# Gathering the chosen tokens with a bfloat16 one-hot matrix and three bfloat16 pieces, split on GpSimd

## The chip, the cores and the metric

The kernel runs on one core of a Trainium2 chip. The metric is device microseconds of one execution, as the median of several runs. The profile is one more execution, taken by the hardware profiler. Engine names in it: PE is the TensorE matmul, PEld its weight load, DVE is VectorE, ACT ScalarE, POOL GpSimd, SP the engine whose queue issues most DMAs.

## The reference, cut to what matters

Four sequences of 512 tokens with 128 features pass through two "layers". The first has three attention parts, two of them with a mixture of eight experts behind them. The second is a block with chosen tokens, four layers of additive attention, and the block with chosen tokens again. The change lies in that block (`k` is 512 / 8 = 64 tokens for each of 8 experts):

```python
logits = sigmoid(einsum('bth,eh->bte', X, Wr))
topk_vals, topk_I = top_k(logits.transpose(0, 2, 1), k)
idx_flat = topk_I.reshape(B, E * k)
Xg = take_along_axis(X, idx_flat[:, :, None], axis=1).reshape(B, E, k, H)
QKV = einsum('beki,eij->bekj', Xg, Wqkv)
Q, K, V = split(QKV, 3)
# rotary angles of the tokens' own places on 64 columns of Q and K
M = topk_I[..., :, None] >= topk_I[..., None, :]
A = softmax(where(M, Q @ K^T / sqrt(128), -inf))
AV = (A @ V) * topk_vals[..., None]
out[b, idx_flat] += AV @ Wo
```

So each expert takes its 64 best tokens out of 512, lets them attend to one another, and adds the result back to the rows that they came from. X is layer-normalized first, and half of the block's output is added to the residual stream.

## The kernel before, in words

Everything is float32 and stays in SBUF. A batch (one sequence) is four chunks of 128 tokens. The work is written as generators, each `yield` a step. `in_turn` and the loops of `first_layer` take steps from several generators in turn, and a scheduler then fixes one order of instructions for each engine. In that order each engine works strictly: an instruction that waits holds up all behind it on its engine. PSUM banks are given out by `bank()` by an estimate of when each comes free.

The block with chosen tokens runs twice: once from about 820 to 980 us of the profile (called the first part below; its beginning overlaps the end of the last mixture of experts) and once from about 1235 us to the end (the last part). Each time, two choices are made, each for two batches at once:

- `choice` (L778 to L856) loads the table `m_trig` (cosines, sines and the token's number) into the columns behind the 128 features of a tile `m_yg` (L785, SP's queue), normalizes X into the tile's first 128 columns (moments L790; `r` on POOL, L154; L182), transposes (L803) and multiplies by the router's weights (L809), forms the sigmoid (`gates`, L819 to L822), transposes it to 16 rows of 512 (L827, L829) and copies it on POOL into the last 8 columns of `m_yg` (L831). So a row of `m_yg` has 201 columns: everything that is to be gathered of a token. Then eight rounds of MAX8 (L836) and MATCH_REPLACE8 (L838) on DVE mark the 64 best, a scan (L846) numbers them, and a transposition (L852, L854) gives `byt`: for each token and expert the slot that it has there, or 0.
- `stream` (L862, one for each batch) makes the one-hot matrix `pick` by comparing `byt` with the slots' numbers (L869, DVE) and gathers by matmul (L880): for each pair of experts and each chunk, `pick` is the stationary operand (128x128) and `m_yg` the moving one (128x201). The gathered rows go to `xs` (L887), are transposed to `xg` (L890), and POOL and DVE take out the chosen token's own gate (`own` L892, `gate` L894). Then come QKV (L903), the rotary part (DVE L915 to L918, POOL's `qk` addition L921 with the tile `other`, two buffers), the transposes of q and k, scores (L931, L932; L932 is the only bf16 matmul of the kernel), softmax, `back` (L952), AV (L961, `av` L964), the output projection (L970) and the one-hot matmul back to the tokens (L983), added to X at L992.
- `chosen_attention` steps both choices and the four streams in turn; a stream starts when its batch is chosen and the stream before it has made five steps.

Beside the first choice of the first part runs the end of the last mixture of experts: `gates` (L673 to L746) computes which two experts a token goes to. In it POOL multiplies and adds two small comparison tables (L712, L718), DVE reduces them to a `rank` (L725) and weights `comb` (L731 to L737), PE transposes those (L741), a DMA puts them to DRAM (L745, `away`) and eight DMAs broadcast them back (L458, `spread`). Each half of an expert is then a matmul (L267), a tanh (L467), a product on DVE (`v`, L472), a product with `spread` on POOL (`hid`, L473) and a second matmul into a sum (L267).

In the last part, the first choice (batches 0 and 1) runs beside the last steps of the additive attention of batches 2 and 3. POOL adds their result to X (L1266), and the second choice's moments (L167) read it.

Of the kernel before, what the change touches and what calls it, by code (L numbers as in the profile page):

```python
# [8 lines left out]
F32 = mybir.dt.float32  # L9
BF16 = mybir.dt.bfloat16  # L10
AF = mybir.ActivationFunctionType
ALU = mybir.AluOpType
AX = mybir.AxisListType

P = 128
B = 4
NC = 4
T = NC * P
# [5 lines left out]
NE = 8  # L24
FH = 2
KSEL = T // 8
# [5 lines left out]
AT_T, AT_G, YG = P + NROT, P + NROT + 1, P + NROT + 1 + NE  # L32
# [8 lines left out]
def tile_macaron(ctx: ExitStack, tc: tile.TileContext, a: dict, out: bass.AP):  # L41
    nc = tc.nc
# [10 lines left out]
    def bank(hold=1.6):  # L53
        i = min(range(8), key=lambda i: free[i])
        free[i] = max(free[i], clock[0]) + hold
        return psum[i].tile([P, T], F32, tag="bank", name="bank")
# [166 lines left out]
    for i in range(4):  # L223
        e = slice(2 * i, 2 * i + 2)
# [7 lines left out]
    def first_layer(opened, picked):  # L232
        with (
# [532 lines left out]
            streaming.close()  # L766
            top = opened()
            choosing = choice([0, 1], lambda b: (1, b) in mixed, top, picked)
            while background or beside or mixing or made:
                halves[0] += 1  # L770
# [7 lines left out]
    def choice(batches, done, top, picked):  # L778
# [1 line left out]

        R = NE * len(batches)
        n = NC * R
        ygs = [top.tile([P, NC, YG], F32, name=f"m_yg{b}") for b in batches]
        for yg in ygs:
            nc.sync.dma_start(yg[:, :, P:AT_G], a["m_trig"].rearrange("(c p) j -> p c j", p=P))  # L785
        while not all(done(b) for b in batches):
# [42 lines left out]
        nc.vector.tensor_copy(left, pr[0:R, :])  # L829
        for i in range(len(batches)):  # L830
            nc.gpsimd.tensor_copy(ygs[i][:, :, AT_G : AT_G + NE], gates[:, :, i * NE : (i + 1) * NE])  # L831
        yield

        for i in range(KSEL // 8):
# [18 lines left out]
        byt = top.tile([P, NC, R], F32, name="byt")  # L853
        nc.vector.tensor_copy(byt, pt[:, 0:n].rearrange("p (c r) -> p c r", c=NC))  # L854
        for i, b in enumerate(batches):
            picked[b] = ygs[i], byt[:, :, i * NE : (i + 1) * NE]  # L856

    def chosen_attention(top, picked, choosing, beside=()):

        with tc.tile_pool(name="moa", bufs=2) as wp:  # L860

            def stream(b):  # L862

                yg, byt = picked[b]

                pick = wp.tile([P, NC, NE, KSEL], F32, name="pick")
                for c in range(NC):
                    at = byt[:, c, :].unsqueeze(2).to_broadcast([P, NE, KSEL])
                    nc.vector.tensor_tensor(  # L869
# [5 lines left out]
                for k in range(2):  # L875
                    ps = bank().rearrange("p (i n) -> p i n", i=2)
                    for i in range(2):
                        r = 2 * k + i
                        for c in range(NC):
                            nc.tensor.matmul(  # L880
                                ps[:, i, 0:YG],
                                lhsT=pick[:, c, 2 * r : 2 * r + 2, :].rearrange("p e s -> p (e s)"),
                                rhs=yg[:, c, :],
                                start=(c == 0),
                                stop=(c == NC - 1),
                            )
                    (nc.scalar.copy if k else nc.vector.tensor_copy)(xs[:, 2 * k : 2 * k + 2, :], ps[:, :, 0:YG])  # L887
                    yield
                xg = wp.tile([P, T], F32, name="xg")
# [9 lines left out]
                for r in range(NPAIR):  # L899
                    ps = bank()  # L900
                    for i in range(2):
                        e = 2 * r + i
                        nc.tensor.matmul(  # L903
                            ps[i * KSEL : (i + 1) * KSEL, 0 : 3 * P],
                            lhsT=xg[:, e * KSEL : (e + 1) * KSEL],
                            rhs=late["m_wqkv"][:, e, :],
                            start=True,
                            stop=True,
# [51 lines left out]
                for r in range(NPAIR):  # L960
                    nc.tensor.matmul(  # L961
                        pav[:, r * P : (r + 1) * P], lhsT=v[:, r, :], rhs=eT[:, r, :], start=True, stop=True
                    )
                av = wp.tile([P, T], F32, name="av")  # L964
                nc.scalar.copy(av, pav)
                yield
                pw = bank()
                for e in range(NE):
# [3 lines left out]
                        lhsT=av[:, e * KSEL : (e + 1) * KSEL],  # L972
                        rhs=late["m_wo"][:, e, :],
                        start=True,
                        stop=True,
# [5 lines left out]
                for c in range(NC):  # L981
                    for r in range(NPAIR):
                        nc.tensor.matmul(  # L983
                            po[:, c * P : (c + 1) * P],
                            lhsT=back[:, r, c * P : (c + 1) * P],
                            rhs=xp[:, r, :],
                            start=(r == 0),
                            stop=(r == NPAIR - 1),
# [3 lines left out]
                nc.vector.scalar_tensor_tensor(X[:, b], by_chunk(po), 0.5, X[:, b], ALU.mult, ALU.add)  # L992

            others = choice([2, 3], lambda b: True, top, picked)
            steps = [0] * B

            def behind(b):

                while b not in picked or (b > 0 and steps[b - 1] < 5):
                    yield  # L1000
                for _ in stream(b):
                    steps[b] += 1
                    yield
                steps[b] += 5
# [101 lines left out]
    def additive_attention(opened, picked, weights, ready):  # L1106

        A = 2 * P
        with tc.tile_pool(name="add", bufs=2) as wp, tc.tile_pool(name="one", bufs=1) as hp:
# [162 lines left out]
            runs += [(STEPS * (i - 1) + 15, weights(i)) for i in range(1, DEPTH)]  # L1272
            top = opened()
            choosing = choice([0, 1], lambda b: b in finished, top, picked)
            last = runs[B - 1][1]
            ended = []
# [16 lines left out]
    with ExitStack() as until_chosen:  # L1293
# [6 lines left out]
        wp, ready = until_done.enter_context(made), {}  # L1300
# [75 lines left out]
```

## Time and profile before

| | |
|---|---|
| time, median of 3 runs | 1371.02 us (1368.14 to 1375.04) |
| the profiled execution's own span | 1369.7 us, 29349 instructions |
| PE busy | 1289.1 us (94%) |
| DVE busy | 954.4 us (70%) |
| ACT busy | 586.5 us (43%) |
| POOL busy | 562.1 us (41%) |
| chain that ended last, by engine | PE 13%, DVE 10%, POOL 4% of the span as merged lines |
| the gather matmuls L880 | 256 records, 0.333 us each by the median, from 888.8 to 1338.3 |

How to read it: the busy time of PE is of modelled ends, and its matmuls overlap, so the time that a matmul takes from PE is the distance between two starts, not its duration. A line of the timeline is: start (us), time until the end of the group (us), engine, line of the kernel, operation, output<-inputs, shapes, count, and in brackets how long the engine sat idle before it and what ended that. A line of the groups is: line, engine, operation, names, shapes, count | busy us, mean ns of one | idle before.

### The profile page before, as it was taken

What the parts mean: (1) busy time and instruction counts of PE and PEld (TensorE: products, weight loads), DVE (VectorE), ACT (ScalarE), POOL (GpSimd) and SP (SyncE); (2) the same over time, 40 slices, a digit from 0 to 9 for tenths busy, and PEclk for the clock granted to TensorE, in tenths of its full rate; (3) what the DMA queues carried; (4) which work ended last, traced back from release to release, by engine and by line L of the source; (5) the groups of instructions that cost most, each with busy time, mean ns of one, the idle gap of its engine ahead of it and who ended that gap; (6) DMA issues with size and microseconds to landing.
All of it is one profiled execution on the core that took longest, in us unless ns stands there. A gap on an engine that the chain in (4) does not pass through costs nothing. (4 is left out here: it accounts for less than half of the span.)

```text
span 1369.7 us, 29349 instructions
## 1 busy us (share of the span) xinstructions
PE 1289.1 (94%) x11050; PEld 699.9 (51%) x11050; DVE 954.4 (70%) x3293; ACT 586.5 (43%) x1180; POOL 562.1 (41%) x823
## 2 busy tenths in 40 slices
PE   5998999999999999999999999989889999997897
PEld 2554445333333333465544443367667767665675
DVE  6886776666658777778767638687466776667773
ACT  1555454454556666665545443222223332323222
POOL 8345655544424112024564755622244443543100
PEclk8999999999999999999999999999979999999799
DMA  3001101020111100000111011211000100000000
GB/s 115 21 24 41 43 33 49 2 80 1 64 45 32 39 1 18 3 19 19 50 33 34 33 53 28 76 40 40 1 20 5 40 1 17 1 1 1 1 9 23
DMA packets 37172, 39.52 MB, mean 29 GB/s; under 512 B 11080, under 2 KB 23880, under 8 KB 37032
## 3 DMA queue, kind: packets, MB, share of 16 engines
q1 hardware_dynamic: 34536, 35.06, 8.3%
q10 hardware_dynamic: 2496, 2.59, 0.6%
q8 instruction: 87, 1.43, 0.4%
q14 instruction: 53, 0.43, 0.1%
HBM read 29.45 MB, written 1.18 MB: 22 GB/s over the span
## 5 line engine op out<-in xcount | busy, mean ns | idle before, releaser
L574 ACT ACTIVATE e<-bank 128x512 f32<-128x512 f32 x576 | 313.7, 595 | 278.4 <-PE bank L527 240.0
L527 PE MATMUL bank<-kA,qA 32*128 32x512 f32 (+3 forms) x1536 | 349.0, 527 | 4.1 <-DVE nm L543 1.8
L562 PE MATMUL bank<-qA,kA 32*128 32x512 f32 (+3 forms) x1536 | 334.0, 524 | 0.3 <-DVE nm L543 0.3
L543 DVE CUSTOM_DVE_ANT_0 junk<-bank,causal 128x384 f32<-128x384 f32 (+3 forms) x512 | 251.0, 490 | 89.5 <-PE bank L527 51.3
L547 DVE TENSOR_REDUCE nm<-bank 128x1 f32<-128x512 f32 x256 | 164.9, 686 | 78.9 <-PE bank L527 78.7
L473 POOL TENSOR_TENSOR hid<-v,spread 128x512 f32<-128x512 f32 x128 | 163.9, 1286 | 127.1 <-DVE v L472 101.7
L562 PEld LDWEIGHTS bank<-qA,kA 32*128 32x128 f32 x1536 | 129.5, 185 | 136.9 <-issue 54.1
L605 PE MATMUL sum<-e,vA 128*32 128x256 f32 (+1 forms) x2560 | 183.7, 368 | 6.1 <-POOL e L580 6.0
L580 POOL TENSOR_SCALAR_AFFINE_SELECT e<-e 128x256 f32<-128x256 f32 x256 | 99.3, 407 | 192.8 <-ACT e L574 191.7
L527 PEld LDWEIGHTS bank<-kA,qA 32*128 32x128 f32 x1536 | 147.4, 187 | 24.6 <-DVE nm L543 5.8
L605 PEld LDWEIGHTS sum<-e,vA 128*32 128x32 f32 x2560 | 62.8, 109 | 165.8 <-issue 134.0
L267 PE MATMUL sum<-hid,sb_f_w 128*32 128x512 f32 x1024 | 135.6, 597 | 3.0 <-POOL hid L473 2.9
L267 PE MATMUL bank<-tT,sb_f_w 128*32 128x512 f32 x1024 | 137.1, 602 | 0.0
L472 DVE SCALAR_TENSOR_TENSOR v<-th,bank 128x512 f32<-128x512 f32 x128 | 87.0, 681 | 43.9 <-ACT th L467 29.2
L467 ACT ACTIVATE th<-bank 128x512 f32<-128x512 f32 x128 | 76.3, 597 | 49.0 <-PE bank L267 39.5
L154 POOL TENSOR_TENSOR r<-v,mhalf 128x4 f32<-128x4 f32 (+1 forms) x64 | 71.8, 1123 | 5.1
L1250 PE MATMUL bank<-h2T,w 128*128 128x512 f32 x128 | 69.0, 632 | 0.2 <-ACT h2T L1239 0.2
L1256 PE MATMUL bank<-w,hid 128*128 128x128 f32 x512 | 65.7, 277 | 0.1
L1256 PEld LDWEIGHTS bank<-w,hid 128*128 128x128 f32 x512 | 63.1, 194 | 4.8 <-issue 1.5
L1251 ACT ACTIVATE hid<-bank,sb_l_cols 128x512 f32<-128x512 f32 x64 | 43.9, 688 | 39.9 <-PE bank L1250 39.8
L1148 PE MATMUL bank<-wa,hT 128*128 128x385 f32 x128 | 56.5, 540 | 1.4 <-ACT hT L1141 1.4
L312 POOL TENSOR_SCALAR v<-mv 128x4 f32<-128x4 f32 x12 | 2.8, 230 | 131.1 <-DVE mv L171 130.8
(279 smaller groups left out, 1805.4 us busy)
## 6 DMA issues: line engine op xcount, KB each, us to landing
spread<-away SPq DMA_DIRECT2D x64, 256.0 KB
qA<-mT SPq DMA_DIRECT2D x192, 2.0 KB
qA<-qC SPq DMA_DIRECT2D x11, 256.0 KB
kA<-kC SPq DMA_DIRECT2D x11, 256.0 KB
w<-in_l_w_dram SPq DMA_DIRECT2D x8, 256.0 KB
sb_m_wqkv<-in_m_wqkv_dram SPq DMA_DIRECT2D x4, 384.0 KB
m_yg<-in_m_trig_dram SPq DMA_DIRECT2D x8, 130.0 KB
X<-in_x_dram SPq DMA_DIRECT2D x4, 256.0 KB
```

Source lines behind the costliest of these rows:

```text
L267: nc.tensor.matmul(ps[32 * j : 32 * j + 32, :], lhsT=w[:, 32 * j : 32 * j + 32], rhs=rhs, start=start, stop=stop, skip_group_check=True,)
L467: nc.scalar.activation(th, ph, AF.Tanh, scale=0.5)
L472: nc.vector.scalar_tensor_tensor(v, th, 1.0, ph, ALU.add, ALU.mult)
L473: nc.gpsimd.tensor_tensor(hid, v, self.spread[e], op=ALU.mult)
L527: nc.tensor.matmul(ps[:, at : at + w], lhsT=t.qA[r0 : r0 + 32, g, c * P : (c + 1) * P], rhs=t.kA[r0 : r0 + 32, g, 0:w], start=True, stop=True,
L543: nc.vector.tensor_tensor_reduce(junk[:, 0:w], src, causal[:, T - w : T], 1.0, NEG, ALU.add, ALU.max, dst)
L547: nc.vector.tensor_reduce(dst, src, axis=AX.X, op=ALU.max)
L562: nc.tensor.matmul(ps[:, at : at + w], lhsT=t.kA[r0 : r0 + 32, g, kc * P : (kc + 1) * P], rhs=t.qA[r0 : r0 + 32, g, q0:T], start=True, sto ...
L574: nc.scalar.activation(es[n][:, j, :], ps, AF.Exp)
L580: nc.gpsimd.affine_select(out=e, in_=e, pattern=[[0, 2], [1, P]], compare_op=ALU.is_ge, fill=0.0, base=0, channel_multiplier=-1,)
L605: nc.tensor.matmul(to[32 * j : 32 * j + 32, q0 + lo - at : q0 + hi - at], lhsT=t.vA[:, kc, 4 * j + g, :], rhs=es[n][:, j, lo:hi], start=fresh,
L1256: nc.tensor.matmul(pm[:, c * P : (c + 1) * P], lhsT=hid[:, f, c * P : (c + 1) * P], rhs=w2[:, f, :], start=(f == 0), stop=(f == 3),)
```

## The change

The gather matmul becomes bfloat16, without loss: each row of `m_yg` is split into three bfloat16 pieces whose sum is the float32 row. The first piece is the row rounded to bfloat16; the rest (float32) is rounded to the second; what is left is the third. `pick` is 0 or 1 and is written as bfloat16. Each f32 matmul becomes three bf16 ones into the same sum.

The split is done on POOL in `choice`, right behind the copy of the gates and ahead of the eight rounds: for each batch and each two chunks (128x402) a conversion, a subtraction, a conversion, a subtraction. `rest` lies in the buffer of `yT` (tag), so a second split of a batch waits for the first. The tiles `m_yg` are now named by their place in a choice and no more by the batch, so the second choice's tiles use the buffers of the first one's and wait until those have been read. The pieces have tiles of their own for each batch. `av` shares the two buffers of `xg`.

In the instruction order of the changed kernel POOL's new operations of the two batches are interleaved with one another and with what POOL did there before.

```diff
-        ygs = [top.tile([P, NC, YG], F32, name=f"m_yg{b}") for b in batches]
+        ygs = [top.tile([P, NC, YG], F32, name=f"m_yg{i}") for i in range(len(batches))]
+        pieces = [[top.tile([P, NC, YG], BF16, name=f"m_p{b}{s}") for s in range(3)] for b in batches]
+
+        def split(i):
+
+            for c in range(0, NC, 2):
+                x, of = [p[:, c : c + 2] for p in pieces[i]], ygs[i][:, c : c + 2]
+                rest = top.tile([P, T], F32, tag=f"yT{i}", name="rest")[:, 0 : 2 * YG].rearrange("p (c n) -> p c n", c=2)
+                nc.gpsimd.tensor_copy(x[0], of)
+                nc.gpsimd.tensor_tensor(rest, of, x[0], op=ALU.subtract)
+                nc.gpsimd.tensor_copy(x[1], rest)
+                nc.gpsimd.tensor_tensor(x[2], rest, x[1], op=ALU.subtract)
+
...
         for i in range(len(batches)):
             nc.gpsimd.tensor_copy(ygs[i][:, :, AT_G : AT_G + NE], gates[:, :, i * NE : (i + 1) * NE])
+        for i in range(len(batches)):
+            split(i)
         yield
...
         for i, b in enumerate(batches):
-            picked[b] = ygs[i], byt[:, :, i * NE : (i + 1) * NE]
+            picked[b] = pieces[i], byt[:, :, i * NE : (i + 1) * NE]
...
-                yg, byt = picked[b]
-
-                pick = wp.tile([P, NC, NE, KSEL], F32, name="pick")
+                pieces, byt = picked[b]
+
+                pick = wp.tile([P, NC, NE, KSEL], BF16, name="pick")
...
                         for c in range(NC):
-                            nc.tensor.matmul(
-                                ps[:, i, 0:YG],
-                                lhsT=pick[:, c, 2 * r : 2 * r + 2, :].rearrange("p e s -> p (e s)"),
-                                rhs=yg[:, c, :],
-                                start=(c == 0),
-                                stop=(c == NC - 1),
-                            )
+                            for k3, piece in enumerate(pieces):
+                                nc.tensor.matmul(
+                                    ps[:, i, 0:YG],
+                                    lhsT=pick[:, c, 2 * r : 2 * r + 2, :].rearrange("p e s -> p (e s)"),
+                                    rhs=piece[:, c, :],
+                                    start=(c == 0 and k3 == 0),
+                                    stop=(c == NC - 1 and k3 == 2),
+                                )
...
-                av = wp.tile([P, T], F32, name="av")
+                av = wp.tile([P, T], F32, tag="xg", name="av")
```

## The prediction, made before the changed kernel had run

> **What bounds it now.** First I read the page's strip of busy tenths, then the timeline around the two places where tokens are chosen (about 815 to 960 us and 1235 us to the end), engine by engine.
>
> ```profile
> span 1369.7 us, 29349 instructions
> PE   5998999999999999999999999989889999997897
> POOL 8345655544424112024564755622244443543100
> ```
>
> TensorE is the bound nearly everywhere, so cheaper gather matmuls should count. GpSimd (POOL) looks half idle. But a queue that is half idle on average can be the one thing waited for in one stage. So next the stage in which the change gives POOL work, the timeline of POOL, DVE and PE after the first choice:
>
> ```profile
> 839.72 0.36 POOL L831 COPY m_yg<-gates 128x32 f32<-128x32 f32 x2
> 840.33 1.27 POOL L473 TENSOR_TENSOR hid<-v,spread 128x512 f32<-128x512 f32 x1 [0.25 <-DVE v L472]
> 841.80 1.27 POOL L473 TENSOR_TENSOR hid<-v,spread 128x512 f32<-128x512 f32 x1 [0.19 <-DVE v L472]
> 844.35 0.73 POOL L712 TENSOR_TENSOR same<-same,before 128x256 f32<-128x256 f32 x1 [1.29 <-DVE same L711]
> 845.16 0.72 POOL L718 TENSOR_TENSOR more<-more,same 128x256 f32<-128x256 f32 x1
> ```
>
> ```profile
> 846.52 0.40 DVE L725 TENSOR_REDUCE rank<-more 128x32 f32<-128x256 f32 x1
> ...
> 852.29 0.17 DVE L737 TENSOR_TENSOR comb<-comb,rs 128x32 f32<-128x32 f32 x1
> ```
>
> ```profile
> 852.51 0.60 PE L741 MATMUL bank<-ident,comb 128*8 128x128 f32 x4 [0.62 <-DVE comb L737]
> ```
>
> The reader is to see a chain: the expert gates of the last mixture pass POOL (L712, L718), then DVE, then PE, then a DMA, and only at 858.75 can POOL multiply its first `hid`. From L831 to L718 POOL idles 1.7 us in all. There is no room for a split there.
>
> **PE: the gather.** 128 f32 matmuls (8 batches x 4 pairs x 4 chunks, two records each) become 384 bf16 ones.
>
> ```profile
> 951.09 3.00 PE L880 MATMUL bank<-m_yg,pick 128*128 128x201 f32 x16
> ...
> 1343.98 0.22 PE L932 MATMUL bank<-paired,ident_h 128*128 128x128 bf16 x1
> 1344.03 0.44 PE L931 MATMUL bank<-kT,qT 128*128 128x128 f32 x2
> ```
>
> Sixteen records need 2.93 us to the next group's start; inside a group a record starts 0.17 us after the other (1335.94, 1336.11, 1336.28), so a matmul takes 0.34. A bf16 matmul of 128 columns has the next one start 0.055 us later; for 201 columns 0.086, three 0.258. Saved: 0.082. The bf16 weight load is a record of 0.10 us against 0.19 for f32, so I count it as hidden under the matmul before it. That is 1.3 us a batch: 2.6 for each two batches at full clock, but 3.3 for the two behind 1277.1, where the first 32 records took 8.29 us at a granted clock of 0.5. Sum 11.2 saved, taken whole, since PE runs without gaps there. Ends: 0.055 a piece (201 columns no dearer than 128) saves 22; 0.17 (no better than an f32 record) costs 22. I take the middle value: the two rows fit one line through their column counts.
>
> A rule weighed against the row: the Trainium skill, "TensorE: Matmul & The Clock Gate", section "Back-to-back issue gap", says that a stream of weight load and matmul pairs at 128 columns sustains about 81 ns each, not the isolated 56. The row here is one bf16 matmul among f32 ones, so it cannot refute that. By the page a piece would be some 111 ns (an estimate), three 0.333, and next to nothing would be saved: +25 instead of the sum below.
>
> **POOL: the split.** Each choice adds 16 operations on 128x402: 8 conversions and 8 subtractions.
>
> ```profile
> L718 POOL TENSOR_TENSOR more<-more,same 128x256 f32<-128x256 f32 x8 | 5.8, 728 | 0.6
> L1266 POOL TENSOR_TENSOR X<-X,Y 128x512 f32<-128x512 f32 x4 | 5.1, 1273 | 10.7 <-DVE Y L1265 10.7
> L112 POOL CAST ident_h<-ident 128x128 bf16<-128x128 f32 x1 | 0.3, 279 | 0.0
> ```
>
> A subtraction lies between 0.728 and 1.273; by width 1.04. A conversion lies between 0.279 and 0.876 (in proportion); with 0.9 ns an element (the one-input select, 292 at 128, 407 at 256) 0.53. Together 12.6 us a choice, ends 8.1 and 17.2. There are four choices. What stands behind them is read from the order of instructions of the changed kernel; each engine runs its own in order.
>
> *A, first choice of the first part.* Thirteen of the 16 (7 conversions, 6 subtractions: 9.95) stand before L712, and one of each plus a `hid` (1.27) between L712 and L718. From L831's end at 840.08: 9.95 + two `hid` 2.54 + 0.73 + 1.04 + 1.27 + 0.53 + 0.73 puts L718's end at 856.9, not 845.9. DVE stands at L725, and behind it the same choice's MAX8/MATCH_REPLACE chain, which fills DVE until 860; PE stands at L741 with the last mixture's 27 hidden matmuls behind it; SP has `away` and eight `spread` loads behind that. One L472 (0.66) has moved ahead: +10. Nothing after it has slack: up to 886 `hid` and v pace it.
>
> *B, first choice of the last part.*
>
> ```profile
> 1256.12 0.36 POOL L831 COPY m_yg<-gates 128x32 f32<-128x32 f32 x2 [2.70 <-DVE gates L822]
> 1261.81 1.26 POOL L1266 TENSOR_TENSOR X<-X,Y 128x512 f32<-128x512 f32 x1 [5.33 <-DVE Y L1265]
> ```
>
> L1266 finishes the last batch's X; now all 16 stand before it: 1256.5 + 12.6 + 1.27 = 1270.4, not 1263.1. DVE takes that batch's statistics (L167, at 1263.52) in the middle of the choice's chain, so the chain waits: +6.9. Also `m_yg0` now serves both choices, so L182 of batch 2, now put into this chain, waits at 1259.7 until the ninth operation has read the tile (1263.3); that is a part of the same 6.9, since DVE still comes to the statistics before POOL does. A wait for `r` (0.9) goes, a yT copy and an L182 piece (1.0) come in: +7. PE idles here already (1263 to 1277).
>
> *C, second choice of the last part.*
>
> ```profile
> 1294.61 0.25 POOL L892 TENSOR_TENSOR own<-xs,mine 128x32 f32<-128x32 f32 x1 [2.40 <-ACT xs L887]
> ```
>
> The second batch's `own` now stands behind all 16, and behind three `qk` adds (1.35). L831 ended at 1285.95; the faster matmuls bring it 1.6 forward; + 12.6 + 1.35 + 0.25 + 0.3 of handovers is 1298.9. DVE's gate reduction (1295.09) waits for it, with the second choice's whole chain to 1315 behind, and the last `qk` add, for which PE's transposes wait. Without the wait it would come at 1295.09 - 3.3, so the wait costs 7.1.
>
> *D, second choice of the first part.* Here `own` and the last `qk` add of the first batch stand early; only the second batch's first `qk` add stands late, behind four conversions and six subtractions (8.4) that follow the first batch's last one. With the matmuls 2.6 ahead, that one ends at 905.6, the late one at 915.1 with handovers, and DVE needs its buffer at 916.7 - 2.6 = 914.1: +1.1.
>
> POOL and DVE also lengthen one another: L182 took 1.34 instead of 0.34 beside L1266, L892 1.68 instead of 0.25 beside L869. The choice's chain did not (MAX8 kept its 0.67 beside L154 at 1268), so I add nothing and leave it to the high ends.
>
> Other edits at nothing: a bf16 `pick` is still one comparison of f32 inputs (0.62 each at L869, PE-covered; if it were dearer DVE has gaps after 1276); `av` in `xg`'s buffers finds them read long before; SP's second m_trig loads wait for the release, about 849 to 855, before `away` comes.
>
> **Sum:** 10 + 7 + 7.1 + 1.1 = 25.2 of waits, less 11.2, is +14. The profiled span of 1369.7 is 1.3 under the median of the runs, 1371.0; on that median: **1385**.
>
> **Rivals.**
> 1. *Faster:* the price of a split operation. If it costs what the smallest rows do (copy 0.21 at L831, `qk` add 0.45), a choice is 5.3 us: A falls to about 3.5, B, C and D to about 0.5 together, against 11.2 saved: -7, 1364. It decides from 5.4 us a choice down. For it: POOL idles most of the time. Against: both rows have far fewer elements.
> 2. *No change:* at the low ends (8.1) the waits are A 5.9, B 2.5, C 2.6, D 0, together 11, and cancel the gain: 1371.
> 3. *The pairs are no faster than f32* (weight loads not hidden): all waits, no gain: 1396; at 0.17 a piece up to 1418.
> At the high ends (17.2) of my own case the waits are 42, +31: 1402.
>
> **Chances.** Forecast 0.68 (1377 to 1402), rival 1 0.07, rival 2 0.15, rival 3 0.10. Half a per cent (about 7 us) is what a measurement of this kernel can tell from no change: faster 0.07, same 0.15, slower 0.78. The range runs from just under rival 2 to the high ends: 1367 to 1402.
>
> **What will show it.** Right: the gather's records start 0.086 apart; a split is 12 to 13 us of POOL; L725 (`rank`) waits some 10 us for POOL, the statistics of the last batch 7, the second gate reduction too; the gather of the first part starts near 899, not 888.8. Wrong: subtractions under 0.7; starts 0.11 or more apart; rank without a wait.

## The result, and the profile after

The changed kernel takes 1393.47 us (1391.79 to 1394.48) against 1369.6 for the kernel before, run on the same chip: a ratio of 1.0169 with a 95% interval of 1.0142 to 1.0195 (formed from the runs; the quotient of the two medians is 1.0174). By the medians that is 23.9 us more, where 14 were forecast (1385.0, range 1367 to 1402).

The page of the kernel after, the lines that answer to those of before. The last one is the group of the experts' second matmuls, with PE's idle time before them at its end; before the change that idle time was 3.0.

```profile
span 1392.0 us, 29686 instructions
...
PE   5998999999999999999999997889799999995788
...
POOL 8345665643432202126464656642145444445400
...
L267 PE MATMUL sum<-hid,sb_f_w 128*32 128x512 f32 x1024 | 138.3, 602 | 12.3 <-POOL hid L473 12.3
```

POOL is a little busier in the slices in which tokens are chosen, and still far from full. PE has new holes in the same slices: the 25th and 26th of 40 (7 and 8 tenths, 9 and 9 before; 835 to 905 us), and deeper ones in the 37th and 38th (5 and 7 tenths, 7 and 8 before; 1253 to 1322 us).

**First part.** The timeline of POOL after the first choice's copy of the gates (line numbers of the changed kernel: L843 is the copy that was L831, L791 to L794 are the split):

```profile
838.47 0.37 POOL L843 COPY m_yg<-gates 128x32 f32<-128x32 f32 x2
838.84 0.99 POOL L791 CAST m_p<-m_yg 128x402 bf16<-128x402 f32 x2
...
845.37 1.25 POOL L473 TENSOR_TENSOR hid<-v,spread 128x512 f32<-128x512 f32 x1
...
850.66 0.71 POOL L712 TENSOR_TENSOR same<-same,before 128x256 f32<-128x256 f32 x1
851.34 0.94 POOL L792 TENSOR_TENSOR rest<-m_yg,m_p 128x402 f32<-128x402 f32 x1
852.25 1.25 POOL L473 TENSOR_TENSOR hid<-v,spread 128x512 f32<-128x512 f32 x1
853.45 0.51 POOL L793 CAST m_p<-rest 128x402 bf16<-128x402 f32 x1
853.93 0.72 POOL L718 TENSOR_TENSOR more<-more,same 128x256 f32<-128x256 f32 x1
```

No line carries a bracket: POOL does not idle from 838.47 on. L718 ends at 854.65, before the change at 845.88. The same stretch on DVE, then on PE:

```profile
854.68 0.42 DVE L725 TENSOR_REDUCE rank<-more 128x32 f32<-128x256 f32 x1 [6.75 <-POOL more L718]
...
859.57 0.17 DVE L737 TENSOR_TENSOR comb<-comb,rs 128x32 f32<-128x32 f32 x1
```

```profile
846.68 1.06 PE L267 MATMUL sum<-hid,sb_f_w 128*32 128x512 f32 x8 [1.81 <-POOL hid L473]
853.55 1.93 PE L267 MATMUL sum<-hid,sb_f_w 128*32 128x512 f32 x8 [5.81 <-POOL hid L473]
856.78 1.93 PE L267 MATMUL sum<-hid,sb_f_w 128*32 128x512 f32 x8 [1.29 <-POOL hid L473]
...
862.84 0.60 PE L741 MATMUL bank<-ident,comb 128*8 128x128 f32 x4
```

DVE waits for L718 as forecast. But `comb` is ready at 859.74, and L741 runs at 862.84 without a bracket: it did not wait for DVE. PE itself was late, because the last `hid` products stand on POOL among the split's operations, and PE waited 8.9 us for three of them. Two chains run through POOL here; the prediction followed that of the gates, and the other one ended last.

**Last part.** POOL, DVE and PE around the first choice of the last part:

```profile
1266.86 0.36 POOL L843 COPY m_yg<-gates 128x32 f32<-128x32 f32 x2 [2.69 <-DVE gates L834]
...
1278.60 1.26 POOL L1281 TENSOR_TENSOR X<-X,Y 128x512 f32<-128x512 f32 x1
```

```profile
1273.22 0.95 DVE L182 TENSOR_SCALAR m_yg<-X,mv,r 128x128 f32<-128x128 f32 x1 [2.84 <-POOL rest L792]
...
1279.90 0.29 DVE L167 BATCH_NORM_STATS2 st<-X 128x6 f32<-128x128 f32 x1 [1.55 <-POOL X L1281]
```

```profile
1285.08 0.47 PE L193 MATMUL bank<-ident,m_yg 128*128 128x128 f32 x1 [6.81 <-DVE m_yg L182]
...
1290.57 3.58 PE L821 MATMUL bank<-sb_m_wr,yT 128*128 128x8 f32 x16 [1.24 <-DVE yT L815]
...
1295.88 5.97 PE L895 MATMUL bank<-m_p,pick 128*128 128x201 bf16 x48 [1.21 <-issue]
```

All 16 operations lie between the two POOL lines: 11.4 us. The addition to X comes last, DVE's statistics wait for it, and in front of them the second choice's normalization (L182) has waited for the split to let go of the shared `m_yg` tile. PE's gather then stands behind the second choice's router matmuls (L821), which waited for the same things. Before the change eight of these sixteen ran early (1263.04), and only eight stood right in front of the gather:

```profile
1273.50 1.88 PE L809 MATMUL bank<-sb_m_wr,yT 128*128 128x8 f32 x8 [0.68 <-ACT yT L803]
...
1277.11 8.29 PE L880 MATMUL bank<-m_yg,pick 128*128 128x201 f32 x32 [1.20 <-issue]
```

The gather starts at 1295.88, 18.77 later than before.

The second choice's split, on POOL, DVE and PE:

```profile
1314.00 0.45 POOL L936 TENSOR_TENSOR qk<-qk,other 128x128 f32<-128x128 f32 x1
...
1316.87 0.25 POOL L907 TENSOR_TENSOR own<-xs,mine 128x32 f32<-128x32 f32 x1
1317.88 1.27 POOL L936 TENSOR_TENSOR qk<-qk,other 128x128 f32<-128x128 f32 x1 [0.76 <-DVE other L933]
```

```profile
1317.15 0.19 DVE L909 TENSOR_REDUCE gate<-own 128x4 f32<-128x32 f32 x1 [6.80 <-POOL own L907]
```

```profile
1314.50 0.66 PE L193 MATMUL bank<-ident,qk 128*128 128x128 f32 x4 [3.26 <-POOL qk L936]
...
1319.20 0.69 PE L193 MATMUL bank<-ident,qk 128*128 128x128 f32 x2 [3.26 <-POOL qk L936]
```

DVE waits for `own`, which comes behind all 16 operations. PE waits twice: for the `qk` addition at 1314.00, which stands among the split's operations, and for the last one, which stands behind `own`.

**What got faster.** Where PE runs at full clock:

```profile
1306.94 2.26 PE L895 MATMUL bank<-m_p,pick 128*128 128x201 bf16 x24
1309.04 0.60 PE L839 MATMUL bank<-ident,gates 128*16 128x128 f32 x4
```

24 records take 2.10 us to the next group's start: 0.0875 each, three pieces 0.263. An f32 matmul took 2 x 0.178 (the mean distance of two records in the groups of 16 before). Over 128 matmuls that is 12.0 us that PE no longer needs. The waits above cost more than that.

### The profile page after: what moved, and what is told of

Read it like the earlier page. It is cut to its first block, busy times and chain, and to the rows that moved or that the text cites. A ratio compares the mean times of both kernels' runs of the same rounds, so it can differ in the third digit from the quotient of the medians.

```text
span 1392.0 us, 29686 instructions
## 1 busy us (share of the span) xinstructions
PE 1287.1 (92%) x11178; PEld 691.8 (50%) x11178; DVE 958.6 (69%) x3293; ACT 586.6 (42%) x1180; POOL 607.8 (44%) x887
## 5 line engine op out<-in xcount | busy, mean ns | idle before, releaser
L267 PE MATMUL bank<-tT,sb_f_w 128*32 128x512 f32 x1024 | 140.0, 609 | 0.2 <-DVE byt L868 0.2
```

Source lines behind the costliest of these rows:

```text
L267: nc.tensor.matmul(ps[32 * j : 32 * j + 32, :], lhsT=w[:, 32 * j : 32 * j + 32], rhs=rhs, start=start, stop=stop, skip_group_check=True,)
```

## Theory and rivals

**T1**, the theory of the prediction: POOL works strictly in its order, 16 more operations stand in front of a few that other engines wait for, and each such place (A to D as in the prediction) delays PE by about what the split delays POOL; the gather's gain arrives in full but is smaller. Against it stand: that the cheaper gather gains little, whatever POOL does, since other waits take its place; that the number of operations decides and not their place; and that the shared buffers (`rest` in `yT`'s, `m_yg` for both choices) cost as much as POOL's order. The text quoted in each experiment says what was expected of T1 and of its rival before it ran.

In profiles of single executions, stretches ahead of the change lie up to 3 us apart. A step's cost is therefore read as the change of the distance between the same PE instruction in two traces, from ahead of the step to behind it. Each ratio is against the kernel before, run on the same chip; the experiments ran on several chips, so two of them are better compared by their ratios than by their times.

## The experiments

### The gather alone

```diff
+    halves_of = [const.tile([P, NC, YG], BF16, name="m_p")] * 3
...
+        nc.gpsimd.memset(halves_of[0], 0.5)
...
-        pieces = [[top.tile([P, NC, YG], BF16, name=f"m_p{b}{s}") for s in range(3)] for b in batches]
+        pieces = [halves_of for b in batches]
...
-        for i in range(len(batches)):
-            split(i)
```

> The bf16 gather without the split: the three pieces are one constant tile, filled with 0.5 once at the start, so the gathered values are left out, and POOL has none of the 64 new operations. From the two traces: 16 f32 records took 2.93 us to the next group, 24 bf16 records take 2.10 (0.0875 each), so 16 groups save 13 if every one counts. Theory 1 (the waits in POOL's queue are the whole loss, the gather's gain arrives whole): 1369.6 - 12 = 1358 us (1354 to 1361). Rival 2 (the gather's gain is mostly given back, because the streams wait for POOL and DVE anyway): 1366 (1363 to 1369).

The tiles `m_yg` are named by batch again here.

1361.73 us, ratio 0.9934 (0.9908 to 0.996): -7.3 by the medians, -9.0 by the ratio, between the two theories. In the profile PE's distance to before goes from -2.07 to -5.65 behind the first part (-3.6), loses some 1.5 again at the hand-over to the additive attention (-4.09 at 993), and goes from -6.3 to -11.99 in the last part. So the gain is real and most of it arrives: 7 to 10 of 12 us.

### The split alone

The f32 gather is put back; the split's operations write pieces that nothing reads. `m_yg` is named by batch. Against the changed kernel, among others:

```diff
-            picked[b] = pieces[i], byt[:, :, i * NE : (i + 1) * NE]
+            picked[b] = ygs[i], byt[:, :, i * NE : (i + 1) * NE]
```

> The split on POOL without the bf16 gather: the same 16 operations at the same place, but the gather reads the f32 rows as before and the pieces are read by nobody (the third overwrites the first; the tiles m_yg have a name for each batch again). Theory 1: the changed kernel's 1393.5 plus the 12 that the gather saves there = 1405 us (1399 to 1411), with L718 some 10 us late in the first part and the last X addition some 11 us late in the last part. Rival 2 (gain given back, so the waits are smaller): 1397 (1394 to 1400). Rival 3 (the reuse of two m_yg tiles is what costs in the last part): 1393 to 1398, with no wait of DVE for the last X addition.

1396.5 us, 1.0197 (1.0165 to 1.0229): +27.4, and +25.4 in the profile, below T1's range and inside those of rivals 2 and 3. Rival 2 is right in part, since the gather alone kept 7 to 10 of 12 us. Rival 3 foresaw no wait of DVE for the last X addition; here it waits 2.40 us for it (1284.79), and not at all before. PE's distance to before, step by step: +0.03 ahead of the change, +11.87 where the first gather runs (A 11.8), 18.4 at 975 (D 6.5, of which 2.5 came back by 1250), 21.35 from 15.88 at the gather of the last part (B 5.5, here without shared `m_yg` tiles), and 26.0 from 20.46 (C 5.5). The prediction's sum of waits was 25.2. Added up, the two halves give -7.3 + 27.4 = 20.1 against 23.9 for the whole; with intervals of about 4 us on each, the difference can't be told from nothing.

### The same operations, later

Nothing is taken away: the split is only issued behind L718 in the first part, behind the last addition to X and behind `own` in the last.

```diff
+    ahead = [None]
...
-                nc.gpsimd.tensor_tensor(more, more, same, op=ALU.add)
+                ahead[0] = nc.gpsimd.tensor_tensor(more, more, same, op=ALU.add).ins
...
-        for i in range(len(batches)):
-            split(i)
...
+        with tc.issue_after(ahead[0]):
+            for i in range(len(batches)):
+                split(i)
```

> The whole change, with the same 16 split operations placed later in POOL's queue: issued behind the eight rounds of a choice, and held behind L718 (first choice of the first part), behind the last X addition (first choice of the last part) and behind the second batch's own (second choices). Theory 1 (place in the queue decides): the waits A, B and C go but for some 3 us (the r of the second choice of the last part now stands behind the split) and 1 to 3 us of the qk additions: 1358 + 5 = 1363 us (1358 to 1368). Rival 2 (gather's gain given back): 1370 (1367 to 1374). Rival 4 (POOL's split slows DVE wherever it stands, by sharing memory access): above 1380.

1374.0 us, 1.0038 (1.002 to 1.0056). The same work in another order costs some 18 us less than the change (1.0038 against 1.0169), so place decides over most of the loss. The expected gain over before does not come: the time is outside T1's range and at the upper edge of rival 2's. What is left, on PE in the first part:

```profile
849.49 1.07 PE L268 MATMUL sum<-hid,sb_f_w 128*32 128x512 f32 x8 [2.02 <-POOL hid L474]
...
854.35 1.39 PE L268 MATMUL sum<-hid,sb_f_w 128*32 128x512 f32 x8 [2.96 <-POOL hid L474]
```

These are the two last `hid`, now behind the split: the second chain of A, which the expectation had left out as the prediction had. About 5 us of A remain, and about 5 of B.

### Two pieces at the change's place

The third piece is left out (the gathered rows have about 16 bits): 8 operations a choice, 256 gather matmuls.

```diff
-        pieces = [[top.tile([P, NC, YG], BF16, name=f"m_p{b}{s}") for s in range(3)] for b in batches]
+        pieces = [[top.tile([P, NC, YG], BF16, name=f"m_p{b}{s}") for s in range(2)] for b in batches]
...
-                rest = top.tile([P, T], F32, tag=f"yT{i}", name="rest")[:, 0 : 2 * YG].rearrange("p (c n) -> p c n", c=2)
...
-                nc.gpsimd.tensor_tensor(rest, of, x[0], op=ALU.subtract)
-                nc.gpsimd.tensor_copy(x[1], rest)
-                nc.gpsimd.tensor_tensor(x[2], rest, x[1], op=ALU.subtract)
+                nc.gpsimd.tensor_tensor(x[1], of, x[0], op=ALU.subtract)
```

> The change with two pieces in place of three, at the place of the change: a split is 4 conversions and 4 subtractions (4 x 0.53 + 4 x 0.93 = 5.8 us a choice), the gather two bf16 matmuls for each f32 one; the third piece of the rows is left out. Theory 1: the gather saves 128 x (0.366 - 0.175) = 24; the waits fall by more than half, because POOL had up to 5.3 us to spare in the last part: A 5 to 6, B 1 to 2, C 2, D 0, together 9: 1369.6 - 15 = 1355 us (1348 to 1361). Rival 2: the gather gives 8, the waits 9: 1370 (1366 to 1375).

1366.07 us, 0.9976 (0.9958 to 0.9995): 27 us less than three pieces, yet in the rival's range and not in T1's. Two pieces need 0.175 for 0.356, 23 us less of PE in all. With half of the operations at the same place 3 of these 23 arrive; with the same two pieces placed elsewhere (below) 11 to 13 do.

### Three pieces, placed, with buffers of their own for the batches

Now behind the last `hid`, behind the last addition to X (the second batch's split also behind the choice's `r`), and behind the `qk` additions; `m_yg` is again named by batch. To make room, `eT` shares the buffer of `qT` and `xp` that of `kT`.

```diff
-        ygs = [top.tile([P, NC, YG], F32, name=f"m_yg{i}") for i in range(len(batches))]
+        ygs = [top.tile([P, NC, YG], F32, name=f"m_yg{b}") for b in batches]
...
+        behind = ahead[0]
+        with tc.issue_after(behind):
+            split(0)
...
+        with tc.issue_after(behind), tc.issue_after(last_root[0]):
+            split(1)
...
-                eT = wp.tile([P, NPAIR, P], F32, name="eT")
+                eT = wp.tile([P, NPAIR, P], F32, tag="qT", name="eT")
...
-                xp = wp.tile([P, NPAIR, P], F32, name="xp")
+                xp = wp.tile([P, NPAIR, P], F32, tag="kT", name="xp")
```

> The whole change with three exact pieces, its 16 split operations placed where POOL has a gap: in the first part behind the last two products hid of the mixture (the run with the later split still had 5 us of PE waiting for these two), in the last part the first batch's behind the last X addition and the second batch's behind the r of the second choice, in the second choices behind own and the qk addition traced last; each batch's m_yg has its own tile again (eT and xp share the buffers of qT and kT to make room). Theory 1, refined (whatever stands behind the split in POOL's queue and feeds PE or DVE soon pays, and nothing else does): what the gather alone gave, 1362 us (1359 to 1366), faster than before. Rival 4 (POOL's split slows DVE and the streams wherever it stands): 1370 or more.

1388.67 us, 1.0138 (1.0099 to 1.0177): the largest miss, and in the range of rival 4. The trace has four delays that add up to some 19 us, enough for it without any other cost of POOL's load. A is down to 1.8, but three others are new. DVE and then PE of this kernel:

```profile
1271.54 0.52 DVE L183 TENSOR_SCALAR m_yg<-X,mv,r 128x128 f32<-128x128 f32 x1 [2.48 <-POOL r L155]
```

```profile
1277.58 3.58 PE L822 MATMUL bank<-sb_m_wr,yT 128*128 128x8 f32 x16 [0.79 <-DVE yT L816]
...
1318.47 0.69 PE L194 MATMUL bank<-ident,qk 128*128 128x128 f32 x2 [3.35 <-POOL qk L940]
...
1322.80 0.69 PE L194 MATMUL bank<-ident,qk 128*128 128x128 f32 x2 [3.64 <-POOL qk L940]
```

`r` of the second choice waits behind the first batch's split (B, +4.7, with the router matmuls in front of the gather; that `yT` shares its buffer with `rest` may be why they stand there, this trace does not show it). The split of the second choice fills the gap between two groups of `qk` additions and more, so PE waits for `qk` twice (C, +8). And 4.3 us are lost near the end: with `xp` in `kT`'s buffers the last copy to `kT` comes right behind an `xp` on DVE (1362.76 and 1362.15), where before the change it came ahead of it (1348.84 and 1351.94). That last one is a cost of the experiment, not of the change.

### The same placing with two pieces

The placing and the `m_yg` tiles of the kernel above, without its shared buffers, and

```diff
-        pieces = [[top.tile([P, NC, YG], BF16, name=f"m_p{b}{s}") for s in range(3)] for b in batches]
+        pieces = [[top.tile([P, NC, YG], BF16, name=f"m_p{b}{s}") for s in range(2)] for b in batches]
...
-                nc.gpsimd.tensor_tensor(rest, of, x[0], op=ALU.subtract)
-                nc.gpsimd.tensor_copy(x[1], rest)
-                nc.gpsimd.tensor_tensor(x[2], rest, x[1], op=ALU.subtract)
+                nc.gpsimd.tensor_tensor(x[1], of, x[0], op=ALU.subtract)
```

> The same placement with two pieces in place of three (the third piece of the rows is left out). Theory 1: one more bf16 matmul of each three goes, 128 x 0.0875 = 11.2 us of PE, of which some two thirds arrive, as with the gather alone (8 of 12): 1362 - 7.5 = 1354 us (1350 to 1358). Rival (the streams are by now bound by DVE and POOL, so PE's further gain is lost): 1359 to 1363.

1357.39 us, 0.9908 (0.9873 to 0.9944): as expected, and faster than before. POOL in the first part:

```profile
847.39 0.99 POOL L791 CAST m_p<-m_yg 128x402 bf16<-128x402 f32 x2
...
851.09 1.86 POOL L792 TENSOR_TENSOR m_p<-m_yg,m_p 128x402 bf16<-128x402 f32 x2
857.27 7.75 POOL L474 TENSOR_TENSOR hid<-v,spread 128x512 f32<-128x512 f32 x5 [4.31 <-DMA spread<-away]
```

Eight operations take 5.6 us, and 4.31 are left until `spread` lands. The gap is 9.9 us: 16 operations of 11.2 to 12 don't fit, 8 do. `eT` and `xp` share no buffers here, and two pieces need no `rest`, so this run and the one before it differ in more than the number of pieces.

### Only the first choice placed

Of the change, A alone is undone: the first choice's split goes behind the last `hid`; everything else stays, `m_yg` named by place included.

```diff
+        seen.append(batches)
+        placed = len(seen) == 1
...
-        for i in range(len(batches)):
+        for i in range(0 if placed else len(batches)):
             split(i)
...
+        behind = ahead[0]
+        if placed:
+            with tc.issue_after(behind):
+                split(0)
...
+        if placed:
+            with tc.issue_after(behind), tc.issue_after(last_root[0]):
+                split(1)
```

> The change as it is, but for the first choice of the first part, whose 16 split operations stand behind the last two hid of the mixture (wait A alone undone). Theory 1: the whole of A returns, measured as 11.4 at the gather's start and 12.7 against the stretch before: 1393.5 - 12 = 1382 us (1379 to 1384). Rival (a later wait, D, takes up part of it, since its operations would then be late against an earlier gather): 1386 to 1390.

1387.32 us, 1.012 (1.008 to 1.016): the rival's range, not T1's, but not for the rival's reason. D is as large as in the change (1.9 and 2.0 from 905 to 970 us). The rest is lost before the gather: L741 starts 11.6 us earlier than in the change, and PE keeps 7.4 of them there. SP's queue and then POOL tell why:

```profile
853.47 0.38 SPq L801 DMA_DIRECT2D m_yg<-in_m_trig_dram  x1
853.90 0.40 SPq L747 DMA_DIRECT2D away<-gT  x1
857.09 0.39 SPq L801 DMA_DIRECT2D m_yg<-in_m_trig_dram  x1
857.60 1.84 SPq L460 DMA_DIRECT2D spread<-away  x4
```

```profile
861.63 7.72 POOL L475 TENSOR_TENSOR hid<-v,spread 128x512 f32<-128x512 f32 x5 [3.01 <-DMA spread<-away]
```

The second choice's table load into the shared `m_yg` tile waits for the split to read the tile (POOL's last reading ends at 857.06), and stands on SP's queue between `away` and `spread`. `spread` is issued at 857.60; in the kernel before it was at 855.27, in a trace that runs 2.0 us later there, so it comes 4.3 us late. A buffer shared by name has put a chain of three queues together: POOL, SP, POOL.

### Only the names

The change with `m_yg` named by batch, and the two shared buffers of the first placing, which make room for it.

```diff
-        ygs = [top.tile([P, NC, YG], F32, name=f"m_yg{i}") for i in range(len(batches))]
+        ygs = [top.tile([P, NC, YG], F32, name=f"m_yg{b}") for b in batches]
...
-                eT = wp.tile([P, NPAIR, P], F32, name="eT")
+                eT = wp.tile([P, NPAIR, P], F32, tag="qT", name="eT")
...
-                xp = wp.tile([P, NPAIR, P], F32, name="xp")
+                xp = wp.tile([P, NPAIR, P], F32, tag="kT", name="xp")
```

> The change as it is, but each batch's m_yg has its own tile as before (eT and xp share the buffers of qT and kT to make room), so that the second choice's normalization no longer waits until the split has read the first choice's tile. The prediction counted this wait as nothing of its own (part of B): 1393.5 (1392 to 1395). Rival: it cost the 2.5 us by which B was 8.0 in the changed kernel and 5.5 in the run of the split alone, which has the separate tiles: 1391 (1389 to 1392).

1392.27 us, 1.0165 (1.0127 to 1.0202): not to be told from the change. The trace tells them apart. B is 5.4 here (from 15.47 to 20.88 at the gather), as in the split alone (5.5), and 8.0 in the change and in each of the three other runs that have the same split and the shared `m_yg` there. So the shared name costs 2.6 us of B. What hides it in the time: 1.6 us are lost near the end (24.7 to 26.4), as in the first placing, which shares `eT`'s and `xp`'s buffers in the same way, and 1.5 between the first part's gather and the last part, for which no reason is shown.

### Three pieces, placed again

`rest` moves to the buffer of `sg`, `xp` to that of `e_`, and the splits follow one another behind `r`.

```diff
-                rest = top.tile([P, T], F32, tag=f"yT{i}", name="rest")[:, 0 : 2 * YG].rearrange("p (c n) -> p c n", c=2)
+                rest = top.tile([P, T], F32, tag="sg", name="rest")[:, 0 : 2 * YG].rearrange("p (c n) -> p c n", c=2)
...
+        behind = ahead[0]
...
+        with tc.issue_after(behind), tc.issue_after(last_root[0]):
+            done_0 = split(0)
+        with tc.issue_after(done_0):
+            split(1)
```

> Three exact pieces, the split placed once more: traced behind the eight rounds and the scan, held behind the last two hid (first part), behind the r of the second choice (last part), behind own (second choices), first batch before second; each batch's m_yg has its own tile, rest lies in the buffer of sg, not in that of yT, so that the second choice's yT waits for no split; eT shares the buffers of qT and xp those of the exponentials. The runs before left 5 us in front of the last part's gather (r and yT waiting for the split), 8 us at the second choice's qk additions and 4 us at the end (kT behind xp, which shared its buffers). Theory 1: with these gone, the gather alone's 1361.7 plus 2 (first hid still behind the split), 2 and 2 (qk additions of the two second choices): 1367 us (1363 to 1371). Rival (a change in POOL's load itself costs, whatever waits): 1378 or more.

1375.54 us, 1.0048 (1.003 to 1.0065): 13 us better than the first placing, between the two ranges, and not below before. PE:

```profile
1281.77 3.42 PE L900 MATMUL bank<-m_p,pick 128*128 128x201 bf16 x18 [1.75 <-POOL rest L793]
...
1312.57 0.90 PE L194 MATMUL bank<-ident,qk 128*128 128x128 f32 x3 [4.79 <-POOL qk L941]
```

The router matmuls no longer stand whole in front of the gather, and B is down to between 2 and 4 us. But at C a `qk` addition still comes 4.8 us late behind the last of the split, and A keeps 2.7. Three exact pieces did not fit into POOL's gaps in any order tried.

### Two pieces, placed again

The same placing with two pieces, no shared buffers.

```diff
+                end = nc.gpsimd.tensor_tensor(x[1], of, x[0], op=ALU.subtract).ins
+            return end
...
+        behind = ahead[0]
...
+        with tc.issue_after(behind), tc.issue_after(last_root[0]):
+            done_0 = split(0)
+        with tc.issue_after(done_0):
+            split(1)
```

> The same placement with two pieces (the third is left out): 5.8 us of split a choice fit all gaps. Theory 1: 1357.4 of the earlier placement less the wait for r and for the qk additions, 1 to 4: 1355 us (1352 to 1358). Rival: 1357 or more, the earlier placement having had no wait left.

1358.68 us, 0.9917 (0.9898 to 0.9935), in the rival's range. The gain of the first such run repeats; the new placing adds nothing to it.

### The change without one choice's split

For the second choice of the first part (D), then for the second choice of the last part (C), constant pieces are gathered and that choice's split is left out.

```diff
+        chosen.append(batches)
+        left_out = len(chosen) == 2
+        if left_out:
+            pieces = [[m_pc] * 3 for b in batches]
...
-        for i in range(len(batches)):
-            split(i)
+        if not left_out:
+            for i in range(len(batches)):
+                split(i)
```

(`== 4` for C.)

> The change without the split of one choice, the second one of the first part (wait D): its pieces are a constant tile, so that choice's gathered values are left out; all else as in the change. The prediction's D, 1.1 us: 1392.4 us (1391 to 1394). Theory 1 with D as the traces show it (the qk additions late by 4 in the changed kernel, by 4.7 to 6.5 in the run of the split alone, some 1 to 2 of it given back before the additive attention): 1393.5 - 4 = 1389.5 (1388 to 1391).

> The change without the split of the second choice of the last part (wait C), in the same way. The prediction's C, 7.1 us: 1386.4 us (1385 to 1388). Theory 1 with C as the trace shows it (the distance to the kernel before grows from 15.2 at 1311 us to 24.5 at 1340, part of it because TensorE's clock falls while it waits): 1393.5 - 9.5 = 1384 (1382 to 1385).

Without D's split 1391.33 us, 1.0164 (1.0148 to 1.0179): 2.1 less than the change by the medians, 0.7 by the ratios, and the intervals overlap, so the times alone don't show D. The time lies in the range given for the prediction's own D. In the profile the distance to the change goes from +0.11 to -3.58 behind the part, and -2.4 at the end. Without C's split 1382.5, 1.0104 (1.0086 to 1.0122), in T1's range: 11.0 less by the medians, 8.9 by the ratios; in the profile from +2.1 to -6.7, so 8.8. DVE of the second kernel at the place where the change waited 6.80:

```profile
1312.41 0.16 DVE L918 TENSOR_REDUCE gate<-own 128x4 f32<-128x32 f32 x1
```

The wait is gone, with nothing in its place.

## Why the prediction was right, and where it was short

The direction and the cause were right: POOL's order, at the four places named. The time was short by 8.5 us and the step by 9.9 (14 forecast, 23.9 measured); the two differ because the kernel before came out at 1369.6 and not at 1371.0. In the profiles the step from before to after is 23.9 (from -1.27 ahead of the change to +22.59 at the end; the medians also give 23.9).

| step | predicted | in the profile of after | by itself |
|---|---|---|---|
| A, first choice of the first part | 10 | 12.7 (-1.27 to +11.44 at the gather) | 11.8 in the split alone |
| B, first choice of the last part | 7 | 8.0 (10.74 to 18.77) | 5.4 and 5.5 with separate `m_yg` |
| C, second choice of the last part | 7.1 | 7.8, net of the gather's gain there (16.5 to 24.3) | 8.8 (profile), 8.9 (ratios), 11.0 (medians) |
| D, second choice of the first part | 1.1 | 3.1 (11.0 to 14.1), partly returned | 2.4 (profile), 0.7 (ratios), 2.1 (medians) |
| gather | -11.2 | spacing gives -12.0 | -9.9 (profile), -9.0 (ratios), -7.3 (medians) |

With 12.7, 8.0, 8.8, 2.4 and -9.9 the sum is 22.0 of 23.9. No single step failed: each is 1 to 3 us dearer than its term, and the gain that arrives a little smaller. What most of this is, the last point of the list says.

- **The price of a split.** Predicted 0.53 a conversion, 1.04 a subtraction, 12.6 a choice. Seen: 0.52 and 0.95 by the median (0.92 into bf16), and 11.4 in a stretch with nothing between. The reading through the nearest rows was good; the low ends (rival 1, 5.3 a choice; rival 2, 8.1) fall with it. The Trainium skill, "GPSIMD Engine Reference", section 3.1 "Elementwise — side-by-side cycle accounting", has 4497 ns for a two-input f32 operation of 2048 elements; in proportion that is 0.88 for 402 (an estimate), near the 0.95 here.
- **A.** L718 was predicted to end at 856.9; it ended at 854.65, or 855.9 with the 1.27 that this execution was ahead. The wait of DVE was predicted as some 10 us and was 6.75, and the gather of the first part starts at 900.2 (predicted near 899). The path fits only in part. "DVE stands at L725 ... PE stands at L741" is true, but PE had its own, longer hold, the `hid` products among the split's operations (1.81, 5.81 and 1.29 us). By the gates alone L741 would have been 8.6 us late (`comb` is ready at 859.74 instead of 852.46, and 1.27 ahead), by PE it was 11.6; that the forecast 10 lies between them is luck. The experiment that moved the split behind L718 alone kept about 5 us for just this reason.
- **B.** Predicted as one chain, X's addition, statistics, the choice. It is that, and a second one: all sixteen router matmuls of the second choice now stand right in front of the gather on PE and wait for `yT` and `m_yg`. The step said of `m_yg` that its wait "is a part of the same 6.9"; the runs give 8.0 with the shared tile and 5.4 without (the change with other names, and 5.5 in the split alone), so it was not: 2.6 of the 8.0 are its own, and the rest is less than the forecast 7. That 7 comes near 8.0 is in part luck.
- **C.** The gate reduction's wait came out as described (6.80; POOL's `own` ends 21.2 behind the gather's start, predicted 21.7). PE's wait for the last `qk` addition was named too. What was left out is an equal wait ahead of it (3.26 each), for the `qk` addition at 1314.00 among the split's operations, and that a waiting PE also slows down, as below.
- **D.** Predicted from one buffer, 1.1; 2 to 3 in the traces, the right order; the times can't tell it from nothing.
- **Gather.** "Three 0.258": 0.263; the 0.34 for an f32 matmul was a little low (2 x 0.178). Rival 3 (pairs no faster than f32) falls. At full clock a pair takes 87.5 ns here, with a weight load for each. The Trainium skill, "TensorE: Matmul & The Clock Gate", section "Back-to-back issue gap", has 81 ns a pair at 128 columns, from which the prediction made 111 for 201. That scaling was wrong: the same sentence of the page has 131 ns at 512 columns, and a line through its two figures gives about 90 at 201 (an estimate), near what was measured. So the page did not speak against the change. That the saving was "taken whole" was too much: the experiment with the gather alone keeps 7 to 10 of 12.
- **No term for the clock.** The prediction left it to the high ends that POOL and DVE lengthen one another; that PE's clock falls when it waits, it doesn't say. The windows view gives the stretches of A, B and C, bounded by the same PE instructions in both traces, first of after, then of before. Each row has the window, its length, PE's busy time, and as the third number from the end the granted clock of PE (PEclk):

```profile
834.73:900.21 65.48, 52.44 (x396) 16.15 (x396) 38.79 (x81) 14.80 (x27) 44.52 (x47) 0.90 0.13 38
1269.04:1295.88 26.84, 10.00 (x48) 7.46 (x48) 18.24 (x46) 2.26 (x4) 12.38 (x17) 0.62 0.05 10
1309.04:1343.25 34.21, 23.78 (x141) 16.25 (x140) 23.75 (x61) 6.85 (x25) 11.15 (x18) 0.80 0.00 0
```

```profile
836.00:888.77 52.77, 48.65 (x397) 15.92 (x396) 37.78 (x81) 14.98 (x27) 33.48 (x31) 1.00 0.12 41
1258.30:1277.11 18.81, 7.71 (x45) 6.10 (x45) 16.24 (x42) 2.25 (x4) 2.52 (x3) 0.69 0.00 0
1293.84:1318.55 24.71, 21.84 (x137) 15.56 (x136) 23.48 (x61) 6.35 (x23) 3.45 (x6) 0.86 0.00 1
```

The three stretches are 12.7, 8.0 and 9.5 us longer, 30.2 in all. PE sits idle for 22.2 of these, where A, B and C were forecast at 24.1; for the other 8.0 it is busy longer with nearly the same work. The clock falls from 1.00 to 0.90, 0.69 to 0.62 and 0.86 to 0.80. So a wait of PE is paid twice here, once while it lasts and once in slower matmuls behind it: eight second matmuls of an expert took 1.93 us behind the wait of 5.81 and 1.06 ahead of it (first part above; the granted clock was 0.5 from 849 to 862 us, and 1.00 throughout that stretch before). These 8.0 us are most of the 9.9 that the forecast missed. This is a reading of two traces, in which the ends of matmuls are modelled; no run takes the fall of the clock away by itself.

## What to carry to other kernels

Before work is given to an engine because it is half idle, look at its queue at the very place where the work would stand: what stands behind it, who waits for that, and how long the longest gap is that ends before it (here 9.9 us: 8 operations fit, 16 don't). A buffer shared by tag or name is a wait across engines, and what is behind it on the waiting queue, a DMA on SP or a matmul on PE, pays too. A wait of PE is to be priced with the slower matmuls behind it (here some 8 us beside 22 of idle time). And the number of pieces is to be counted against the precision that is needed: two pieces, placed behind the last product that others wait for, gave 0.9908 and 0.9917 of the time before, three exact ones 1.0038 at best.

## What the runs showed of the hardware that was not expected

- Weight load and matmul pairs in bf16 keep 0.0875 us a pair at 201 columns at full clock. At the start of the last part, behind PE's idle time, 48 of them took 5.80 us to the next group's start (0.121 each); the granted clock was 0.5 until 1299.
- DVE's operations on 128x128 took 0.95 instead of 0.32 us at 1273 (L182), beside a split on POOL, and 0.60 to 0.61 for the next two; the choice's MAX8 on 16 partitions kept its 0.68.
- POOL's conversion to bf16 is the cheaper half: 0.52 against 0.95 for a subtraction of the same 128x402. But single conversions took up to 1.29 us (at 920.32).
